# A graph layer's gather split between GpSimd and TensorE, with a maximum every second batch and direct stores

## The chip, the cores and the metric

The kernel runs on one core of one Trainium2 chip. The metric is device time in microseconds: the median of the runs. The kernel before takes 3633.04 us (3632.4 to 3636.79, three runs).

## The reference

Two graph layers, each followed by a layer norm; 6250 nodes with 16 features, 200000 edges sorted by destination. The change concerns the second layer:

```python
def _L1_gnn_ref(feat, efeat, W_msg, b_msg, W_attn, b_attn, src, dst):
    w_m = (efeat @ W_msg + b_msg).reshape(E, in_f, -1)
    w_a = (efeat @ W_attn + b_attn).reshape(E, in_f, -1)
    h_src = feat[src][:, :, None]
    e1 = w_m * h_src
    e2 = w_a * h_src
    seg_max = jax.ops.segment_max(e2, dst, num_segments=N)
    ex = jnp.exp(e2 - seg_max[dst])
    denom = jax.ops.segment_sum(ex, dst, num_segments=N)
    attn = ex / denom[dst]
    ft = jax.ops.segment_sum(e1 * attn, dst, num_segments=N)
    return ft.sum(axis=1)
```

`feat` is the first layer's output, x1 in the kernel (6272 x 16 with padding). Per edge there are two 16x16 matrices made from its attributes, each multiplied by the source node's row.

## The kernel before, in words

The first layer (to about 1600 us) is a loop over 196 batches of 1024 edges, one-hots and matmuls; the change adds only small work ahead of it. `update` then makes x1 and writes it to DRAM.

The second layer works on 197 batches of eight tiles of 128 edges, two tiles from each of four stretches of the edge list (S = 4). Its steps, each a small function:

- `gather(b)` (L579): eight indirect DMAs on GpSimd (L587), one a tile, fetch the source rows from x1 in DRAM into `hb`, two batches ahead (LEAD = 2).
- `load(b)` (L592): the edge attributes of two batches, on SP's queue.
- `multiply(b,u)` (L605): TensorE makes both matrices of two tiles in `pw` (two fp32r matmuls of 66x512, L613). There are three `pw` buffers, so it waits for `product` of three steps earlier.
- `maxima(b,u)` (L621): VectorE multiplies the attention half by the rows and takes the largest value of each partition into `cm`. `exps` (L628): ScalarE, exp of that minus a reference value, `neg[b]`. `message` (L632) and `product` (L637): VectorE, the other half times the rows, times the exp.
- `hot(b,..)` (L641): ScalarE makes one-hots of the destination within a window of R = 32 nodes, eight activations and one Relu.
- `add(b,0)` and `add(b,1)` (L681): TensorE adds the tiles into `acc` by the one-hots (L689, four windows side by side), and the carry from the batch before (L687).
- `leave(b)` (L692): ScalarE copies `acc`, of which there is one, to `sums`. `invert(b)` (L697): Ln and Exp on ScalarE, 1/denominator, written to `bank[:, 256:512]` (L701). `fold(b)` (L703): VectorE multiplies and reduces to 16 features per node.
- The reference value, every batch: `highest` (L652), VectorE; `across` (L656), a transpose on TensorE into `bank`; `top` (L659), VectorE, a maximum over it with the last `top`; `spread` (L667), TensorE, to all partitions; `refer` (L670), ScalarE, into `neg`; `carry` (L674), the factor between the two references.
- `store` (L713) and `put` (L718): every two batches the sums go to a DRAM log, and from there four DMAs a batch carry 32 nodes each to two tables at places read from a register. All are on SP's queue, and each `put` waits for the one before it on its table.

`bank` is one tile of PSUM of 512 columns, which `across`, `top`, `spread`, `refer`, `invert` and `fold` share in different ranges.

The order is written out by hand (L766 to L836), and each engine works through it in that order. In pass b the loop issues `new` work of batch b, `add` of batch b-1, and `leave`, `invert`, `fold` of batch b-2. On ScalarE the order is: leave, exps 0, invert, exps 1, hot 0-2, exps 2, refer, carry, hot 3-5, exps 3, hot 6-7. On TensorE: multiply 0, across, multiply 1, multiply 2, add 0, spread, multiply 3, add 1. On VectorE: maxima 0, message 0, maxima 1, top, message 1, product 0, maxima 2, message 2, product 1, maxima 3, message 3, product 2, fold, highest, product 3.

Three passes (12, 14, 16) also hold tests of the input (`checks`), each some 5 us. If one of these tests, or one at the end (`far_off`), finds that the assumptions on the data don't hold, a flag starts a slow general path.

Of the kernel before, what the change touches and what calls it, by code (L numbers as in the profile page):

```python
# [27 lines left out]
G = 8  # L28
# [4 lines left out]
S = 4  # L33
R = 32
LEAD = 2
RING = 16384
# [6 lines left out]
@with_exitstack  # L43
def gnn_kernel(ctx, tc, x_q, x_t4, src_p, dst_p, src_w, dst_w, prev_w, dst_r, base_h, src_q, dst_q, base_q, ea8_w, ea16, ea16_t,
               w_tp4, bd_w, w1_4, w1_msg, b1_msg, w1_attn, b1_attn, out):
# [16 lines left out]
    eas_dram = dram.tile([32, EP], F32, name="eas_dram")  # L62
    end_dram = dram.tile([32, 2 * W], F32, name="end_dram")
    tabs = [dram.tile([NP + W, D], F32, name=f"tab{k}_dram") for k in range(2)]

# [52 lines left out]
    with ExitStack() as l0:  # L118
# [24 lines left out]
        with tc.tile_pool(name="tab", bufs=2) as tabp, tc.tile_pool(name="tab1", bufs=1) as tab1, \  # L143
# [25 lines left out]
            for r in (16, 48):  # L169
# [14 lines left out]
                lambda: nc.vector.tensor_scalar(nsb, sb, -1.0, None, OP.mult),  # L184
            ]
            xhs = {}

# [303 lines left out]
    dwf, pwf, dqf, bqf = (t.bitcast(F32) for t in (dwi, pwi, dqi, bqi))  # L491
    step = keep.tile([W, NM], F32, name="step")

    def stretches():

        nc.vector.tensor_copy(dqf, dqi)
        nc.vector.tensor_copy(bqf, bqi)
        nc.vector.tensor_tensor(nrw.rearrange("p (m k) -> p m k", k=2), bqf.unsqueeze(2).to_broadcast([W, NM, 2]),
                                dqf.rearrange("p (m k) -> p m k", k=2), OP.subtract)
        nc.vector.memset(step[:, 0:S], -1000.0)  # L500
        nc.vector.tensor_tensor(step[:, S:NM], bqf[:, S:NM], bqf[:, 0:NM - S], OP.subtract)
        nc.vector.tensor_scalar(shiftw, step, float(R), 1000.0, OP.is_ge, OP.mult)
        nc.vector.tensor_tensor(step, step, shiftw, OP.add)
        sv = step.rearrange("p (b s) -> p b s", s=S)
        nc.vector.tensor_tensor(sv, sv, foot.unsqueeze(1).to_broadcast([W, NQ, S]), OP.add)
        nc.vector.tensor_scalar(shiftw, step, chan, None, OP.is_equal)

    def in_order():
# [14 lines left out]
    def fit_second():  # L523

        nc.vector.tensor_scalar(dqf, nrw, -float(R), None, OP.is_le)
        nc.vector.tensor_reduce(bad[:, 1:2], dqf, AX.X, OP.max)

        nc.vector.memset(step[:, 0:2 * S], 0.0)
        nc.vector.tensor_tensor(step[:, 1:S], bqf[:, 1:S], bqf[:, S + 1:2 * S], OP.is_equal)
        nc.vector.tensor_reduce(bad[:, 5:6], step[:, 0:S], AX.X, OP.max)  # L530
        nc.vector.tensor_tensor(step[:, S:2 * S - 2], bqf[:, 2:S], bqf[:, 1:S - 1], OP.subtract)
        nc.vector.tensor_scalar(step[:, S:2 * S - 2], step[:, S:2 * S - 2], R + 1.0, None, OP.is_le)
        nc.vector.tensor_reduce(bad[:, 6:7], step[:, S:2 * S - 2], AX.X, OP.max)
# [26 lines left out]
    with ExitStack() as l1:  # L560
        xp = l1.enter_context(tc.tile_pool(name="l_x", bufs=3))
        wp = l1.enter_context(tc.tile_pool(name="l_w", bufs=3))
        logp = l1.enter_context(tc.tile_pool(name="log", bufs=4, space=DRAM))
        psw = l1.enter_context(tc.tile_pool(name="l_psw", bufs=3, space=PSUM))
# [7 lines left out]
        x1n = keep.tile([W, NP // W, D], F32, name="x1n")  # L572
        nc.sync.dma_start(out=x1n, in_=x1_dram.rearrange("(p c) d -> p c d", p=W))
        checks = {12: in_order, 14: fit_first, 16: fit_second}
        st = {}

        bank = psm.tile([W, 512], F32, name="bank")

        def gather(b):  # L579

            st[b] = {"hb": []}
            st.pop(b - 8, None)
            for u in range(G // 2):
                hb = hp.tile([W, 2, D], F32, name="hb")
                for k in range(2):
                    t = b * G + 2 * u + k
                    nc.gpsimd.indirect_dma_start(  # L587
                        out=hb[:, k, :], out_offset=None, in_=x1_dram[:, :],
                        in_offset=bass.IndirectOffsetOnAxis(ap=srcq[:, t:t + 1], axis=0))
                st[b]["hb"].append(hb)  # L590

        def load(b):  # L592
# [6 lines left out]
            for r in (0, 32):  # L599
                to = ev[r:r + 32, :].bitcast(F32)  # L600
                nc.sync.dma_start(out=to.rearrange("r (s n) -> r s n", s=S)[:, 0:part.shape[1], 0:part.shape[2]], in_=part)
                if b == NQ - 1:
                    nc.sync.dma_start(out=to[:, (S - 1) * 4 * W:(S - 1) * 4 * W + 2 * W], in_=end_dram)

        def multiply(b, u):  # L605
# [46 lines left out]
        def highest(b):  # L652
            st[b]["m1"] = wp.tile([W, 1], F32, name="m1")
            nc.vector.tensor_reduce(st[b]["m1"], cm[:, b * S:(b + 1) * S], AX.X, OP.max)

        def across(b):  # L656
            nc.tensor.transpose(bank[0:1, 0:W], st[b]["m1"], ident)  # L657

        def top(b):  # L659

            before = st[b - 1]["top"] if b > 0 else None
            st[b]["top"] = wp.tile([1, 1], F32, name="top")
            nc.vector.tensor_reduce(st[b]["top"], bank[0:1, 0:W], AX.X, OP.max)
            if before is not None:
# [4 lines left out]

        def refer(b):  # L670

            nc.scalar.activation(neg[:, b:b + 1], bank[:, W:W + 1], AF.Copy, scale=-1.0)

        def carry(b):  # L674

            gap = wp.tile([W, 1], F32, name="gap")
            nc.scalar.activation(gap, neg[:, b - 1:b], AF.Exp, scale=-1.0, bias=neg[:, b:b + 1])
            nc.scalar.activation(cols[b % 3].rearrange("p (s r) -> p s r", r=R)[:, :, 0], shiftw[:, b * S:(b + 1) * S],
# [24 lines left out]
        def fold(b):  # L703
            v = st[b]
            r = wp.tile([W, 256], F32, name="q")
            nc.vector.tensor_tensor(r, bank[:, 256:512], v["sums"][:, 256:512], OP.mult)
            if b % 2 == 0:
                v["ft"] = wp.tile([W, 2, D], F32, name="ft")
            else:
                v["ft"] = st[b - 1]["ft"]  # L710
            nc.vector.tensor_reduce(v["ft"][:, b % 2, :], r.rearrange("p (i o) -> p o i", i=D), AX.X, OP.add)

        def store(b):  # L713

            st[b]["lg"] = lg = logp.tile([2, S, R * D], F32, name="lg")
            nc.sync.dma_start(out=lg.rearrange("k s (r d) -> (s r) k d", d=D), in_=st[b]["ft"])

        def put(b):  # L718

            rvs = nc.values_load_multi_w_load_instructions(  # L720
                bases_q[0:1, b * S:(b + 1) * S], engines=(mybir.EngineType.SP,), min_val=0, max_val=6249,
                skip_runtime_bounds_check_because="every dst is one of the 6250 nodes")[1]
            for s, rv in enumerate(rvs):
                if b < NQ - 3:
                    n, part = R, st[b | 1]["lg"][b % 2, s:s + 1, :]
                    nc.sync.dma_start(out=tabs[s % 2][ds(rv, n), :].rearrange("r d -> (r d)").unsqueeze(0), in_=part)
                else:
                    n = R if b < NQ - 1 else 1
                    nc.sync.dma_start(out=tabs[s % 2][ds(rv, n), :], in_=st[b]["ft"][s * R:s * R + n, b % 2, :])

        def clear():
# [4 lines left out]
            for s in range(1, S):  # L736
                rv = nc.values_load(bases_q[0:1, s:s + 1], engines=(mybir.EngineType.SP,), min_val=0, max_val=6249)
                nc.sync.dma_start(out=tabs[(s - 1) % 2][ds(rv + 1, R), :], in_=none)
                nc.sync.dma_start(out=tabs[s % 2][ds(rv, 1), :], in_=none[0:1, :])
# [11 lines left out]
        with tc.issue_after(tables.ins):  # L751
            for b in range(LEAD):
                gather(b)
            with tc.manual_schedule(engines=ORDERED | {mybir.EngineType.SP}):
# [8 lines left out]
                spread(0)  # L763
                refer(0)
                refer(1)
                for b in range(NQ + 2):  # L766
                    new, old, gone = b < NQ, 1 <= b <= NQ, b >= 2
                    trail = old and b + 1 < NQ
                    if b + LEAD < NQ:
                        gather(b + LEAD)  # L770
                    if b % 2 == 0:
                        if 2 <= b and b + 2 < NQ:
                            load(b + 2)
                        if 4 <= b and b - 3 < NQ - 3:
                            put(b - 4)
                            put(b - 3)
                    if new:
# [17 lines left out]
                    if new:  # L795
                        message(b, 1)
                        multiply(b, 2)
                        product(b, 0)
                    if old:
# [10 lines left out]
                    if trail:  # L810
                        refer(b + 1)
                    if b + 1 < NQ:
                        carry(b + 1)
                    if new:
                        hot(b, 3, 6)
                        maxima(b, 3)
                        exps(b, 3)
                        message(b, 3)
                        product(b, 2)
                        hot(b, 6, G)  # L820
                    if old:
                        add(b - 1, 1)
                    if gone:
                        fold(b - 2)
                        if b - 2 >= NQ - 3:
                            put(b - 2)
                        elif b % 2:
                            store(b - 2)
                    if new:
                        highest(b)  # L830
                        product(b, 3)
# [375 lines left out]
```

## Time and profile before

| | |
|---|---|
| median of three runs | 3633.04 us |
| the profiled execution: its own time | 3637.97 us |
| its span, first to last instruction | 3636.2 us |
| mean granted TensorE clock | 0.757 |
| busy: TensorE, VectorE, ScalarE, GpSimd | 3216.4, 3260.0, 2789.1, 1880.2 us |
| second layer, 1644.88 to 3586.24 us (194 batches): TensorE, VectorE, ScalarE, GpSimd busy | 1771.1, 1750.8, 1358.9, 1464.0 us of 1941.4 |
| mean clock there | 0.61 |
| gathers L587 | 1576, mean 946 ns |

The page shares busy time over the whole span, and the two layers differ much: the granted clock is 0.9 and more in nearly every slice of the first and 0.5 to 0.6 in the second. A busy TensorE at half clock needs twice the time for the same columns, so its busy time is to be read beside the clock. Stretches of single batches tell more than the sums. "Releaser" is what ended the idle time before an instruction.

### The profile page before, as it was taken

The page shows a single profiled execution, that of the slowest core. Times are in us where ns is not written, and L with a number is a line of the kernel's source. Part 1 is how long each engine was busy: PE and PEld are TensorE (multiplying, and loading weights), DVE is VectorE, ACT ScalarE, POOL GpSimd, SP SyncE. Part 2 cuts the span into 40 slices and gives each one's busy share as a digit, 9 for nine tenths or more (in the row PEclk, how much of TensorE's full clock was granted, in tenths as well). Part 3 has the DMA queues.
Part 4 walks back from the last instruction along what each step waited for, and adds up shares of the span by engine and source line. Part 5 has one row for each costly group of instructions (what it writes and reads, how often), then busy time and mean ns, then how long its engine had stood idle before and what let it go on. Part 6 is the DMA issues. An engine that isn't in the chain of part 4 may idle for free.

```text
span 3636.2 us, 53067 instructions
## 1 busy us (share of the span) xinstructions
PE 3216.4 (88%) x13725; PEld 2042.5 (56%) x13725; DVE 3260.0 (90%) x6470; ACT 2789.1 (77%) x5393; POOL 1880.2 (52%) x1792
## 2 busy tenths in 40 slices
PE   3999999999999999849799999999999999989995
PEld 3999989999999998823233333333333333333331
DVE  5999999999999999778989999999999998998986
ACT  4999999999999999716666777777777776776764
POOL 0222222222222222317777777777777777777773
PEclk9999999999999999955656666666665665565655
DMA  5433333333333333231121221212212122221211
GB/s 179 134 122 123 115 123 121 118 117 124 123 122 109 125 124 117 88 64 27 31 38 32 38 38 32 38 33 37 38 32 38 32 38 37 33 38 32 38 32 28
DMA packets 258415, 264.55 MB, mean 73 GB/s; under 512 B 105269, under 2 KB 193910, under 8 KB 258107
## 3 DMA queue, kind: packets, MB, share of 16 engines
q1 hardware_dynamic: 205931, 241.66, 22.8%
q0 software_dynamic: 50432, 13.01, 4.1%
q10 hardware_dynamic: 1744, 6.41, 0.6%
q8 instruction: 115, 1.88, 0.2%
q14 instruction: 193, 1.58, 0.1%
HBM read 223.67 MB, written 38.64 MB: 72 GB/s over the span
## 4 chain that ended last, share of the span: by engine, by line
PE 70%; DVE 14%; issue 7%; DMA 4%; ACT 3%; POOL 1%; SPq 0%; ACTq 0%; POOLq 0%; DVEq 0%
PE acc L348 32%; PE pw L613 13%; PE acc L689 12%; PE acc L687 6%; PE pm L283 5%; DVE xs L639 4%; DVE xs L624 3%; DVE pw L635 2%; DMA hb<-x_dram,srcq 2%; PE bank L668 1%; POOL hb L587 1%; ACT bank L701 1%; ACT r L700 1%; DMA xw_dram<-hl 1%; PE bank L657 1%
## 5 line engine op out<-in xcount | busy, mean ns | idle before, releaser
L587 POOL DMA_INDIRECT hb<-x_dram,srcq x1576 | 1490.4, 946 | 557.4 <-issue 269.4
L329 POOL TENSOR_TENSOR ll<-oa,sl 128x1024 fp32r<-128x1024 f32 x196 | 380.1, 1939 | 1146.1 <-DVE sl L336 1088.0
L630 ACT ACTIVATE xs<-xs,neg 128x512 f32<-128x512 f32 x788 | 562.6, 714 | 477.9 <-DVE cm L624 477.9
L613 PE MATMUL pw<-w,ev 66*128 66x512 f32 x1584 | 762.6, 610 | 77.7 <-DVE xs L639 59.7
L306 ACT ACTIVATE away<-iota,nsb 128x784 f32<-128x784 f32 x784 | 699.1, 939 | 5.9 <-DVE nsb L184 0.4
L689 PE MATMUL acc<-xs,oh 128*32 128x512 f32 x3152 | 687.7, 961 | 0.7 <-ACT sums L695 0.7
L613 PEld LDWEIGHTS pw<-w,ev 66*128 66x128 f32 x1584 | 375.0, 280 | 465.8 <-issue 340.4
L624 DVE CUSTOM_DVE_ANT_1 xs<-pw,hb 128x512 f32<-128x512 f32 x792 | 537.9, 679 | 91.0 <-PE pw L613 78.7
L308 ACT ACTIVATE oba<-away,one_t 128x3136 fp32r<-128x3136 f32 x196 | 572.7, 2922 | 6.4
L635 DVE TENSOR_TENSOR pw<-pw,hb 128x512 f32<-128x512 f32 x788 | 547.1, 694 | 20.5
L639 DVE TENSOR_TENSOR xs<-pw,xs 128x512 f32<-128x512 f32 x788 | 533.4, 677 | 0.0
L316 DVE TENSOR_SCALAR obd<-iota,sb 128x784 fp32r<-128x784 f32 x784 | 454.6, 622 | 0.0
L647 ACT ACTIVATE away<-iota,nrw 128x32 f32<-128x32 f32 x1576 | 389.6, 306 | 0.0
L348 PE MATMUL acc<-obd,ll 128*128 128x392 f32 x1568 | 346.6, 366 | 0.0
L687 PE MATMUL acc<-sums,col 128*128 128x512 f32 x392 | 340.6, 968 | 0.0
L348 PE MATMUL acc<-oba,ll 128*128 128x392 f32 x1568 | 326.1, 352 | 0.0
L283 PE MATMUL pm<-tw,ot 128*128 128x128 f32 x1568 | 214.5, 282 | 113.5 <-issue 89.9
L348 PE MATMUL acc<-obd,lh 128*128 128x392 f32 x1568 | 312.7, 341 | 1.0 <-DVE lh L329 1.0
L348 PE MATMUL acc<-oba,lh 128*128 128x392 f32 x1568 | 312.8, 341 | 0.0
L348 PEld LDWEIGHTS acc<-oba,ll 128*128 128x128 f32 x1568 | 298.8, 198 | 0.0
L689 PEld LDWEIGHTS acc<-xs,oh 128*32 128x32 f32 x3152 | 76.5, 135 | 382.7 <-issue 300.3
L348 PEld LDWEIGHTS acc<-obd,ll 128*128 128x128 f32 x1568 | 291.2, 202 | 0.0
(149 smaller groups left out, 3517.6 us busy)
## 6 DMA issues: line engine op xcount, KB each, us to landing
db<-in_dst_r SPq DMA_DIRECT2D x196, 512.0 KB
ev<-eas_dram SPq DMA_DIRECT2D x196, 256.0 KB
hb<-x_dram,srcq POOLq DMA_INDIRECT x1576
tw<-xw_dram SPq DMA_DIRECT2D x784, 32.0 KB
er<-in_ea_t SPq DMA_DIRECT2D x28, 448.0 KB
eas_dram<-eh SPq DMA_DIRECT2D x28, 448.0 KB
eas_dram<-el SPq DMA_DIRECT2D x28, 448.0 KB
tab_dram<-lg SPq DMA_DIRECT2D x776, 2.0 KB
```

The source lines that it names most:

```text
L306: nc.scalar.activation(v["away"][:, t, :], iota, AF.Abs, bias=nsb[:, b * G + t:b * G + t + 1])
L308: nc.scalar.activation(v["oba"], v["away"], AF.Relu, bias=one_t, scale=-1.0)
L316: nc.vector.tensor_scalar(v["obd"][:, t, :], iota, sb[:, n:n + 1], None, OP.is_equal)
L348: nc.tensor.matmul(acc[:, s, :B // 2], l[:, t].rearrange("p a h -> p (a h)"), ob[:, s * B // 2:(s + 1) * B // 2], start=b == 0 and t == GA ...
L587: nc.gpsimd.indirect_dma_start(out=hb[:, k, :], out_offset=None, in_=x1_dram[:, :], in_offset=bass.IndirectOffsetOnAxis(ap=srcq[:, t:t + 1 ...
L613: nc.tensor.matmul(pw[:, k].rearrange("p c n -> p (c n)"), ev[:, e:e + W], w1, start=True, stop=True)
L624: nc.vector.tensor_tensor_reduce(over(v["xs"][:, u, 0]), over(v[u][:, :, 0]), rows(b, u), 1.0, -2.0 * BIG, OP.mult, OP.max, cm[:, b * S + ...
L630: nc.scalar.activation(x, x, AF.Exp, bias=neg[:, b:b + 1])
L635: nc.vector.tensor_tensor(m, m, rows(b, u), OP.mult)
L639: nc.vector.tensor_tensor(x[:, u, 1], st[b][u][:, :, 1], x[:, u, 0], OP.mult)
L687: nc.tensor.matmul(v["acc"], cols[b % 3], st[b - 1]["sums"], start=False, stop=False)
L689: nc.tensor.matmul(v["acc"][s * R:(s + 1) * R, :], v["oh"][:, 2 * s + k, :], v["xs"][:, s, :, k, :], start=k == 0, stop=k == 1)
```

## The change

1. **Gather.** From batch 3 (PICK) GpSimd fetches seven tiles; the eighth comes from x1 in SBUF. There x1 lies as eight groups of 7 x 112 nodes: partition = node within 112, column block m (of seven), 8 x 16 columns for the eight groups; as two fp32r parts, `th` and `tl`. `places(b)` loads, on SP's queue, a row of 7 x 128 distances broadcast to 112 partitions (401 KB); `lows(b)` makes the one-hots `ox` of it on ScalarE (Abs and Relu over 112x896) at the end of the pass before; `pick(b)` adds 14 fp32r matmuls of 112x128 weights and 128 columns into `bank[:, 0:128]`; `choose(b)` takes the right one of eight groups on VectorE and writes the rows to `hb`.
2. **Preparation.** Twelve VectorE operations and eight DMAs ahead of the first layer write these distances to DRAM; `stretches` makes the group mask `which_h`; `table` splits x1.
3. **Maximum.** `highest`, `across`, `top`, `spread`, `refer` run every second batch and set two values of `neg`; the reference is up to one batch older. `across` and `top` use `bank[0:1, 128:256]`.
4. **Store.** `put(b-2)` follows `fold(b-2)` and writes 31 nodes (V) a window straight from SBUF; the log and `store` are gone.

The core of the diff:

```diff
+        def places(b):
+
+            xr[b] = xp.tile([X, 7 * W], F32, name="xr", bufs=2)
+            nc.sync.dma_start(out=xr[b], in_=xr_dram[b:b + 1, :].to_broadcast([X, 7 * W]))
+
+        def lows(b):
+
+            nc.scalar.activation(xr[b], xr[b], AF.Abs, bias=nchan[:X])
+            st[b]["ox"] = xp.tile([X, 7, W], F32R, name="ox", bufs=1)
+            nc.scalar.activation(st[b]["ox"].rearrange("p m e -> p (m e)"), xr.pop(b), AF.Relu, bias=one_t[:X], scale=-1.0)
+
+        def pick(b):
+
+            for m in range(7):
+                for k, t in enumerate((th, tl)):
+                    nc.tensor.matmul(bank[:, 0:8 * D], st[b]["ox"][:, m, :], t[:, m, :],
+                                     start=m + k == 0, stop=m + k == 7)
+
+        def choose(b):
+
+            g = wp.tile([W, 8, D], F32, name="g", bufs=2)
+            nc.vector.tensor_tensor(g, bank[:, 0:8 * D].rearrange("p (h d) -> p h d", d=D),
+                                    which_h[:, b, :].unsqueeze(2).to_broadcast([W, 8, D]), OP.mult)
+            nc.vector.tensor_reduce(st[b]["hb"][S - 1][:, 1, :], g.rearrange("p h d -> p d h"), AX.X, OP.add)
...
+            n = V if b < NQ - 1 else 1
             for s, rv in enumerate(rvs):
...
+                nc.sync.dma_start(out=tabs[s % 2][ds(rv, n), :], in_=st[b]["ft"][s * R:s * R + n, :])
...
-                    trail = old and b + 1 < NQ
+                    trail = old and b + 1 < NQ and b % 2 == 0
...
                         multiply(b, 2)
+                        if b >= PICK:
+                            pick(b)
                         product(b, 0)
...
                     if trail:
-                        refer(b + 1)
+                        refer(b + 1, 2)
...
                         hot(b, 3, 6)
+                        if b >= PICK:
+                            choose(b)
                         maxima(b, 3)
...
                         hot(b, 6, G)
+                        if PICK <= b + 1 < NQ:
+                            lows(b + 1)
...
                         fold(b - 2)
-                        if b - 2 >= NQ - 3:
-                            put(b - 2)
-                        elif b % 2:
-                            store(b - 2)
+                        put(b - 2)
+                    if PICK <= b + 2 < NQ:
+                        places(b + 2)
```

## The prediction

> **What bounds the kernel now.** First the engine times by stretch. The second layer's 197 batches begin 1644.88 us into the span (first start of `leave`, L695), and the 194 periods to 3586.24 take 1941.4 us: 10.01 each, or 9.93 without some 15 us of checks at batches 12, 14 and 16. I cut out three batches (start of `maxima(b,0)` to the next):
>
> ```profile
> core 0: us, PE busy (x) PEld busy (x) DVE busy (x) ACT busy (x) POOL busy (x), PEclk, DMA share, GB/s
> 2541.52:2551.71 10.19, 10.19 (x31) 3.90 (x29) 8.98 (x21) 7.02 (x20) 7.69 (x9) 0.50 0.07 7
> 2502.80:2512.26 9.46, 7.21 (x30) 2.53 (x29) 8.89 (x22) 6.91 (x20) 7.25 (x8) 0.80 0.09 9
> 2522.38:2531.93 9.55, 6.03 (x32) 2.39 (x30) 8.98 (x22) 6.92 (x20) 7.11 (x9) 1.00 0.09 8
> ```
>
> There are two regimes. At half clock TensorE is busy for all 10.19 us; at full clock it needs about 6 and VectorE sets 9.5. The mean clock of the 194 periods is 0.61, so most batches are of the first kind. GpSimd is near a third bound: eight gathers, 0.944 each and 0.30 between them, make 9.98 us, and it works almost without a break. But VectorE waits only 2.2 us in all for rows (wait table, 2000 to 3500), so it is a limit just below the other two.
>
> Next the chain in order of time, in a half-clock batch, then the timeline of the batch at 2502.80, where ScalarE and VectorE meet:
>
> ```profile
> 2542.21 1.71 PE pw L613 x4
> 2543.91 1.87 PE acc L689 x8
> 2545.78 0.51 PE bank L668 x2
> 2546.29 1.16 PE pw L613 x2
> 2547.45 1.71 PE acc L687 x2
> 2549.16 1.87 PE acc L689 x8
> 2551.03 1.15 PE pw L613 x2
> ```
>
> ```profile
> 2504.14 0.49 ACT L700 ACTIVATE r<-sums,tiny_t 128x256 f32<-128x256 f32 x1
> 2504.66 0.39 ACT L701 ACTIVATE bank<-r 128x256 f32<-128x256 f32 x1
> 2504.99 0.19 ACT L701 ACTIVATION_READ_ACCUMULATOR bank<-r 128x1 f32 x1
> 2505.20 0.28 DVE L663 TENSOR_REDUCE top<-bank 1x1 f32<-1x128 f32 x1 [0.40 <-ACT bank L701]
> ...
> 2509.49 0.71 ACT L630 ACTIVATE xs<-xs,neg 128x512 f32<-128x512 f32 x1
> 2510.10 0.52 ACT L647 ACTIVATE away<-iota,nrw 128x32 f32<-128x32 f32 x2
> ...
> 2510.65 0.51 ACT L650 ACTIVATE oh<-away,one_t 128x256 f32<-128x256 f32 x1
> 2511.06 0.58 ACT L695 ACTIVATE sums<-acc 128x512 f32<-128x512 f32 x1
> ```
>
> In the first, TensorE has no hole. In the second, `top` waits for `invert`'s write into another range of the same tile `bank`: waits on `bank` hold for the whole tile. And ScalarE passes without a break from `hot` to the next `leave`, which starts 1.2 us ahead of the next `maxima`.
>
> **TensorE: 14 matmuls more.** Nearest row: L283, also fp32r, 128x128 weights and 128 columns, at half and at full clock:
>
> ```profile
> 1085.79 1.94 PE L283 MATMUL pm<-tw,ot 128*128 128x128 f32 x8 [3.19 <-issue]
> 704.63 1.08 PE L283 MATMUL pm<-tw,ot 128*128 128x128 f32 x8
> ```
>
> Within the eight, starts lie 0.213 us apart at half clock and 0.111 at full, so `pick` costs 14 x 0.213 = 2.99 or 14 x 0.111 = 1.56. The Trainium skill (TensorE: Matmul & The Clock Gate, Back-to-back issue gap) gives about 0.081 for a load and matmul pair of 128 columns in a sustained stream: 1.13. I take the row; the rule's 0.4 us goes into the lower end. Halving `across` (0.21) and `spread` (0.51) returns 0.36. TensorE's half-clock batch is 10.19 + 2.99 - 0.36 = 12.8 if nothing else delays it.
>
> **VectorE.** `choose` adds a 128x128 multiply (the 128x256 one of L706 takes 0.413, so about 0.28) and a reduce over it (L711, twice as large, takes 0.584: 0.33 to 0.58); 0.6 to 0.86, I take 0.75. `top` (0.28 + 0.15, in the stream 0.39) and `highest` (0.06) go every second time. Without waits a batch is 9.46 - 0.40 (today's wait) = 9.06 now; then 9.06 - 0.06 + 0.75 = 9.75 for even and 9.06 - 0.39 + 0.75 = 9.42 for odd ones, mean 9.58.
>
> **ScalarE.** `lows` adds two 112x896 activations. L306 (784 elements) takes 0.939, L308 (3136) 2.922: 0.84 ns an element over 0.28, so 1.03 each, 2.06 together. It fits the total (7.0 + 2.06 - about 0.25 for the halved `refer` and `gap`), but the place decides: ahead of `leave`, which frees `acc` and starts `invert`. From `exps(b,3)` to the next `leave` are 2511.06 - 2509.49 = 1.57 now, then 3.63. From that `exps` (start = end of `maxima(b,3)`) to the next `maxima` are 2512.26 - 2509.43 = 2.8. `leave` then starts 0.83 after `maxima` instead of 1.2 before, and `exps(b,0)` waits behind it. I lay the batch out with `maxima` at 0: `leave` 0.83, `exps` 1.4, Ln 2.0, Exp 2.55, both done at X = 3.0 (now 2.4).
>
> **What waits on that.** The built order says what `pick` waits for: in odd batches the Exp of `invert(b-2)`, in even ones `top(b-1)`, which itself waits for that Exp. Queued behind `pick` are `add(b-1,0)`, `spread` and `multiply(b,3)`, which `maxima(b,3)` needs; from `maxima(b,3)` to the next batch are 3.5 us. At full clock (TensorE rows halved):
> - even: VectorE reaches `top` at 2.03, stalls to 3.0 (now 2.4); `pick` 3.35 to 4.95, `add` to 6.0, `spread` 6.4, `refer` 6.6, `choose` to 7.4 (it waits for `refer`), `maxima(b,3)` 7.4, period 10.9.
> - odd: `pick` 3.05 to 4.65, `add` to 5.7, `multiply(b,3)` to 6.45; `maxima(b,3)`, otherwise due at 5.9, starts there; period 10.0.
>
> Mean 10.45. At half clock, with the rows of the chain: even 3.35 + 3.0 + 1.87 + 0.51 + 1.16 = 9.9, and 3.5 more are 13.4; odd 3.05 + 3.0 + 1.87 + 1.16 = 9.1, so 12.6. Mean 13.0.
>
> **Which clock?** It changes in steps of 3.41 us. I added up, for each such step, the time in which matmul columns move. At full clock every step of layer two below 0.45 was followed by half clock (0.23 to 0.38 typically), all with 0.52 or more kept it. At half clock full speed came back after 0.84 and more, in layer one from 0.75; steps around L687 with no `spread` in them. `pick` moves columns only half of its time (0.053 of 0.111). In the full-clock layout TensorE idles from about 0.8, the end of `multiply(b,2)`, to 3.2. A step ending anywhere between 1.5 and 5.3 then has under 0.4; that stretch is longer than a step, so nearly every batch drops the clock once. Half clock then lasts two or three steps, till one lies in the dense part (`add`, `multiply`, L687, `add`, 6.6 us long). Followed by hand: a drop at 1.5 gives a 13.0 batch, the next step boundaries then miss the gap and give 10.4; a drop at 3.6 gives 12.65 and then 11.6. Averages 11.7 and 12.1; I take 11.75. The same page (Part 1) says that a busy step of some 3.4 us brings full clock and that activity releases the throttle: read alone, more matmuls would help, and the loop would run at 10.45. Against that stands the first row above: 10.19 busy of 10.19, and the clock at 0.50.
>
> **The rest.** `gather` loses one of eight: GpSimd 8.73 a batch, no gain while others set 10.4. SP: four direct stores a batch; the tail of today's run has eight such in 11.91 us, so 6 us a batch for four against 2 x 4.4 per two batches now. `places` is queued behind `put` and its fold: issued about 3.5 after the batch's start. The nearest row, db (512 KB broadcast), moves in 2.2 to 2.5 us; with issue and landing about 4, so the 401 KB are there at 7.5, before `lows` at 8.9. If late by 1 us, all of the batch is: +190 us. Layer one's twelve small VectorE operations and seven ACT DMAs (each third waits for a landing, about 8 us) lie in a hole: VectorE waits 12.3 us there for the first `pm`. `table` and its seven loads: 0 to +5 at the start of layer two; six operations in `stretches` (3.2 us) in a 4.0 us wait for rows. The tail has four stores less after the last fold: 0 to -6. Sum taken as 0.
>
> **Sum.** 194 x (11.75 - 9.93) = +353 us. The profiled execution is 3637.97 (span 3636.2 and 1.8 around it), so 3991; the median of the runs lies 4.9 below: 3986.
>
> **Rivals.**
> - Clock stays full (chance 0.20): 194 x 0.52 = +101: 3734. For it: `pick` fills part of today's gap. Against: half its time moves no columns, and `lows` moves the gap rather than closing it.
> - Clock stays half (0.14): 194 x 3.07 = +596: 4229. For it: today's 0.61. Against: 13 us is not near three steps (10.24) as 10.19 is, so the boundaries walk quickly into the dense part.
> - Faster (0.05): the waits on `bank` and behind `lows` vanish in other slack at full clock, VectorE's 9.58 sets the pace, GpSimd's 9.98 being gone: -68, 3565. It decides if `pick` starts by about 2.4 rather than 3.0 and the clock holds; the row 2511.06 (ScalarE has no gap there) speaks against it.
> - The change doesn't do what it says (0.01): a window over 31 nodes or a maximum two batches old sets the flag, and the general path runs, far outside any range. Destinations rise slowly, so I leave it.
> - The mixed clock (0.60): 3986, own range 3840 to 4140.
>
> The range 3730 to 4230 takes in full and half clock up to their middles. Beyond 0.2%, about what a measurement tells from no change: faster 0.05, same 0.02, slower 0.93.
>
> **What would show it.** Right: batches of 10 to 13.4 us with a mean near 11.75, the clock falling once in most batches during the gap before `pick`; `leave` starting behind the 112x896 pair, after `maxima(b,0)`; even batches longer than odd ones by 0.8, with VectorE waiting about 1 us at `top`; `pick` 1.6 or 3.0 long; GpSimd idle about 3 us a batch. Wrong: a steady clock over 0.9, `pick` starting right behind `multiply(b,2)`, or ScalarE waiting for `xr`.

## The result and the profile after

| | before | after |
|---|---|---|
| median of four runs each, one chip | 3632.72 us (3629.86 to 3636.79) | 4186.85 us (4179.08 to 4194.52) |
| span of the profiled execution | 3636.2 | 4177.3 |
| mean clock, all / second-layer loop | 0.757 / 0.61 | 0.786 / 0.687 |
| 194 periods of `leave`, total, mean | 1941.4, 10.01 | 2487.5, 12.82 |

The ratio is 1.153, 95% interval 1.151 to 1.154. The profiled execution grew by 541.1 us: the loop by 546.1, and what lies around it shrank by 5.0. So all of the loss is in the batches, at 2.8 us each, while the mean clock went up.

The runs in the last part of the experiments were made on three chips where the kernel before itself takes 4181 to 4189 us, so they are compared only with each other.

First the groups of the page, with mean duration and, behind the second bar, the idle time ahead of them:

```profile
L632 POOL DMA_INDIRECT hb<-x_dram,srcq x1382 | 1305.5, 945 | 1272.7 <-DVE pw L709 899.8
L669 PE MATMUL bank<-th,ox 112*128 112x128 f32 x1358 | 476.0, 368 | 380.2 <-DVE top L737 216.7
L698 DVE CUSTOM_DVE_ANT_1 xs<-pw,hb 128x512 f32<-128x512 f32 x792 | 540.8, 683 | 317.7 <-PE pw L687 309.5
```

GpSimd now waits for buffers (900 us): it is no limit. TensorE stands idle for 380 us ahead of `pick` (L669), 2 us a batch. VectorE waits 310 us for matmuls in `pw`. Next the stretches: an even and an odd batch, then one of the rare full-clock ones:

```profile
core 0: us, PE busy (x) PEld busy (x) DVE busy (x) ACT busy (x) POOL busy (x), PEclk, DMA share, GB/s
2801.14:2813.85 12.71, 10.43 (x44) 4.88 (x43) 9.66 (x24) 9.78 (x24) 6.59 (x7) 0.73 0.38 80
2813.85:2825.88 12.03, 10.48 (x43) 5.26 (x41) 9.35 (x22) 7.67 (x21) 6.60 (x7) 0.72 0.16 39
2022.81:2032.76 9.95, 7.30 (x43) 3.58 (x41) 9.23 (x22) 8.19 (x21) 6.42 (x7) 1.00 0.20 46
```

The same work takes 9.95 at full clock and 12 to 12.7 at a mean clock of 0.72. Before, a batch was either all slow with TensorE busy throughout, or nearly all fast. Now no engine is busy throughout, and hardly a batch is of either kind. The timeline of the even batch (maxima at 2801.14) shows how it begins:

```profile
2799.89 1.03 ACT L661 ACTIVATE xr<-xr,nchan 112x896 f32<-112x896 f32 x1
2800.96 1.04 ACT L663 ACTIVATE ox<-xr,one_t 112x896 fp32r<-112x896 f32 x1
2801.91 0.57 ACT L771 ACTIVATE sums<-acc 128x512 f32<-128x512 f32 x1
...
2803.52 0.39 ACT L777 ACTIVATE bank<-r 128x256 f32<-128x256 f32 x1
2803.84 0.19 ACT L777 ACTIVATION_READ_ACCUMULATOR bank<-r 128x1 f32 x1
2804.06 0.28 DVE L737 TENSOR_REDUCE top<-bank 1x1 f32<-1x128 f32 x1 [0.91 <-ACT bank L777]
...
2804.40 0.33 PE L669 MATMUL bank<-th,ox 112*128 112x128 f32 x1 [2.28 <-DVE top L737]
```

`leave` (L771) follows the pair of `lows` (L661, L663), 0.77 us after the maxima; the Exp is done at 2.9; `top` waits 0.91 for it; `pick` starts at 3.26 behind a hole of 2.28. TensorE's own rows of the odd batch, maxima at 2813.85, show what comes of it:

```profile
2816.30 0.33 PE L669 MATMUL bank<-th,ox 112*128 112x128 f32 x1 [1.55 <-ACT bank L777]
...
2818.83 0.41 PE L669 MATMUL bank<-tl,ox 112*128 112x128 f32 x1
2819.17 1.94 PE L765 MATMUL acc<-xs,oh 128*32 128x512 f32 x8
2821.04 1.22 PE L687 MATMUL pw<-w,ev 66*128 66x512 f32 x2
2822.05 1.73 PE L763 MATMUL acc<-sums,col 128*128 128x512 f32 x2
2823.72 1.06 PE L765 MATMUL acc<-xs,oh 128*32 128x512 f32 x8
```

The eight matmuls of `add` take 1.94 (half clock) right behind `pick` and 1.06 (full clock) at the end of the pass. By the trace's record of the clock, which changes in steps of 3.41 us, it fell at 2816.65, 0.35 us into `pick`, and rose at 2823.48. In between lies the serial stretch `pick`, `add`, `multiply(b,3)`, which `maxima(b,3)` waits for, and the carry (L763):

```profile
2819.28 0.29 DVE L675 TENSOR_TENSOR g<-bank,which_h 128x128 f32<-128x128 f32 x1 [0.15 <-PE bank L669]
2819.60 0.37 DVE L677 TENSOR_REDUCE hb<-g 128x16 f32<-128x128 f32 x1
2822.30 0.69 DVE L698 CUSTOM_DVE_ANT_1 xs<-pw,hb 128x512 f32<-128x512 f32 x1 [2.32 <-PE pw L687]
```

`choose` is short; then VectorE stands for 2.32 us. Cut at `maxima(b,0)`, over batches 12 to 189, in us and mean granted clock:

| kernel | batches | `pick` starts | `maxima(b,3)` | from there to next | period | clock in the gap | clock from `pick` to `maxima(b,3)` |
|---|---|---|---|---|---|---|---|
| changed | even | 3.20 | 9.14 | 4.40 | 13.54 | 0.98 | 0.59 |
| | odd | 2.51 | 8.54 | 3.64 | 12.17 | 0.91 | 0.53 |
| e1, Exp to SBUF | even | 2.36 | 9.15 | 4.61 | 13.76 | 0.65 | 0.50 |
| | odd | 0.96 | 6.52 | 3.70 | 10.22 | - | 0.83 |
| e4, `pick` later | even | 3.89 | 7.69 | 3.71 | 11.40 | 0.82 | 0.71 |
| | odd | 2.97 | 6.59 | 4.00 | 10.59 | 0.89 | 0.76 |
| e8, hole filled | even | 3.24 | 7.42 | 3.66 | 11.08 | 1.00 | 1.00 |
| | odd | 3.68 | 9.37 | 3.70 | 13.07 | 0.79 | 0.58 |

("Gap" is from 0.8 us after the batch's start to `pick`; in e1's odd batches it is hardly there and has no figure.) In the changed kernel the clock is full in the gap, where nothing runs, and near half where the batch's end is decided. In batches 12 to 189 it falls 168 times, and 166 of the 178 batches have a fall: 146 lie ahead of `pick` or within it, 20 between it and `maxima(b,3)`, two later.

What precedes each fall? The next table takes the 3.41 us ahead of each fall in the same batches, and names the matmuls ahead of which TensorE stood idle longest there (holes over 0.1 us):

| kernel | falls | longest hole ahead of |
|---|---|---|
| changed | 168 | `pick` 168 |
| e1, Exp to SBUF | 89 | `across` 57, `pick` 30, `multiply` 2 |
| e2, `lows` in mid-pass | 121 | `pick` 93, `multiply` 28 |
| e4, `pick` later | 95 | `spread` 44, `add` 30, `multiply` 10, `across` 9, `pick` 2 |
| e8, hole filled | 74 | `multiply` 74 |

In the changed kernel it is always the hole ahead of `pick`. Each later edit takes away part of these falls, and in what is left another hole comes first.

### The profile page after: what moved, and what is told of

The parts are those of the page before. It is cut to its first block, busy times and chain, and to the rows that moved or that the text cites. A ratio compares the mean times of both kernels' runs of the same rounds, so it can differ in the third digit from the quotient of the medians.

```text
span 4177.3 us, 58353 instructions
## 1 busy us (share of the span) xinstructions
PE 3539.7 (85%) x16147; PEld 2426.6 (58%) x16147; DVE 3368.4 (81%) x6583; ACT 3119.4 (75%) x5585; POOL 1695.2 (41%) x1598
## 4 chain that ended last, share of the span: by engine, by line
PE 67%; ACT 19%; DVE 6%; issue 6%; DMA 2%; POOL 0%; SPq 0%; ACTq 0%; DVEq 0%; POOLq 0%
PE acc L373 28%; PE bank L669 12%; PE acc L765 11%; PE pw L687 7%; PE pm L308 5%; ACT xs L704 4%; ACT ox L663 3%; DVE xs L698 3%; ACT xr L661 3%; PE acc L763 2%; ACT bank L777 2%; ACT r L776 2%; ACT sums L771 2%; ACT away L721 1%; PE bank L742 1%
## 5 line engine op out<-in xcount | busy, mean ns | idle before, releaser
L632 POOL DMA_INDIRECT hb<-x_dram,srcq x1382 | 1305.5, 945 | 1272.7 <-DVE pw L709 899.8
L669 PE MATMUL bank<-th,ox 112*128 112x128 f32 x1358 | 476.0, 368 | 380.2 <-DVE top L737 216.7
L765 PE MATMUL acc<-xs,oh 128*32 128x512 f32 x3152 | 669.4, 936 | 0.8 <-ACT sums L771 0.8
L687 PE MATMUL pw<-w,ev 66*128 66x512 f32 x1584 | 627.3, 515 | 22.2 <-DVE cm L698 17.4
L669 PEld LDWEIGHTS bank<-th,ox 112*128 112x128 f32 x1358 | 370.0, 272 | 467.2 <-DVE top L737 258.6
L687 PEld LDWEIGHTS pw<-w,ev 66*128 66x128 f32 x1584 | 313.3, 233 | 484.3 <-issue 410.1
L669 PE MATMUL bank<-tl,ox 112*128 112x128 f32 x1358 | 474.9, 365 | 0.0
L669 PEld LDWEIGHTS bank<-tl,ox 112*128 112x128 f32 x1358 | 380.4, 280 | 0.0
L763 PE MATMUL acc<-sums,col 128*128 128x512 f32 x392 | 352.1, 998 | 0.0
```

What stands on the lines that cost most here:

```text
L632: nc.gpsimd.indirect_dma_start(out=hb[:, k, :], out_offset=None, in_=x1_dram[:, :], in_offset=bass.IndirectOffsetOnAxis(ap=srcq[:, t:t + 1 ...
L669: nc.tensor.matmul(bank[:, 0:8 * D], st[b]["ox"][:, m, :], t[:, m, :], start=m + k == 0, stop=m + k == 7)
L687: nc.tensor.matmul(pw[:, k].rearrange("p c n -> p (c n)"), ev[:, e:e + W], w1, start=True, stop=True)
L765: nc.tensor.matmul(v["acc"][s * R:(s + 1) * R, :], v["oh"][:, 2 * s + k, :], v["xs"][:, s, :, k, :], start=k == 0, stop=k == 1)
```

## The experiments

Theory T: `pick` waits, through the shared tile `bank`, for an Exp that is late behind `lows`; the hole ahead of it drops the clock, and the serial stretch behind runs at half clock. Rivals: R1, the sheer load of 14 more matmuls; R2, the two ScalarE operations in front of `leave`; R3, the other parts of the change.

### The chip of 3631 us: one edit at a time

These four ran together; the kernel before took 3631.4 us beside them.

**e1: the Exp out of the shared tile.**

```diff
-            nc.scalar.activation(bank[:, 256:512], r, AF.Exp, scale=-1.0, accum_out=rsum[:, b:b + 1])
+            v["inv"] = r
+            nc.scalar.activation(r, r, AF.Exp, scale=-1.0, accum_out=rsum[:, b:b + 1])
...
-            nc.vector.tensor_tensor(r, bank[:, 256:512], v["sums"][:, 256:512], OP.mult)
+            nc.vector.tensor_tensor(r, v["inv"], v["sums"][:, 256:512], OP.mult)
```

> Edit: invert(b-2) writes its Exp into an SBUF tile instead of bank[:, 256:512]; all else as in the changed kernel (4187 us, batches of 12.82). In odd batches pick then waits only for the one-hots of lows, in even ones for top, which no longer waits for the Exp. Theory T (pick is late because of the shared tile, the hole before it drops the clock, and the serial stretch pick, add, spread, multiply(b,3) then runs at half clock): pick starts near 1.0 after maxima(b,0) in odd and 2.4 in even batches instead of 2.5 to 3.3; mean batch 10.8, 3800 us (3700 to 4000). Rival R1 (14 more matmuls on a TensorE that runs at half clock, 12.8 us of work a batch, wherever they wait): 12.4 to 12.8 a batch, 4110 to 4190. Rival R2 (two ScalarE operations ahead of leave, nothing else): leave stays late, 4187.

Measured: 4012.42 us, 1.105 of the kernel before (1.103 to 1.107); mean batch 11.97. That is 12 us above T's band and 98 below R1's, but the batches part. An even and an odd batch of this kernel, and the hole that ends the odd one:

```profile
core 0: us, PE busy (x) PEld busy (x) DVE busy (x) ACT busy (x) POOL busy (x), PEclk, DMA share, GB/s
2797.20:2810.94 13.74, 12.84 (x43) 6.66 (x42) 9.59 (x23) 9.99 (x24) 7.14 (x8) 0.51 0.34 73
2810.94:2820.55 9.61, 7.08 (x43) 3.68 (x41) 9.27 (x22) 7.45 (x20) 6.08 (x7) 1.00 0.16 48
```

```profile
2820.09 0.27 PE L731 MATMUL bank<-ident,m 128*1 128x128 f32 x1 [2.43 <-DVE m L728]
```

Both have the same 14 matmuls. In the odd one `pick` starts at 0.96 (mean), as T says; there the clock recovers, and the batch takes 9.61. In the even one, where `pick` still waits for `top` and starts at 2.36, TensorE is at half clock, busy for 12.84: the 12.8 of R1. So the load counts in full once the clock is half. What brings half clock here is mostly not the hole that T named: at the end of a full-clock odd batch TensorE stands for 2.43 us ahead of `across` (L731), waiting for `highest` (L728), and the clock falls at 2820.87, right behind. The Exp in `bank` is worth 174 us; the hole ahead of `across` took the place of the one ahead of `pick`.

**e2: `lows` in mid-pass.**

```diff
+                        if PICK <= b + 1 < NQ:
+                            lows(b + 1)
                         hot(b, 3, 6)
...
-                        if PICK <= b + 1 < NQ:
-                            lows(b + 1)
```

(With two buffers for `ox` and, for room, one for `q`.)

> Edit: lows(b+1) moves from the end of the pass to between carry and hot(b,3,6), so that leave and invert follow hot directly as in the kernel before. Theory T: leave starts about 1 us ahead of maxima(b,0) again, Exp of invert is done at 2.2 to 2.4 instead of 2.9, pick starts 0.5 to 0.9 earlier; the hole of TensorE stays over 1.4 us, so the clock still falls in most batches: 12.0 to 12.3 a batch, 4030 to 4090 us. R2 (the place of lows is the whole loss): the 2.06 us come back, 10.7 a batch, 3790. R1 (sheer TensorE load): no change, 4150 to 4190.

Measured: 4126.9 us, 1.137 (1.135 to 1.139); mean 12.52. `pick` starts at 2.76 and 2.44 instead of 3.20 and 2.51, and even batches' `top` waits 0.40 again instead of 0.91, but the clock still averages 0.69 and 0.50 from `pick` to `maxima(b,3)`. 60 us come back, somewhat less than T's 100 to 160 and far from R2's 400. R2 falls, also because e4 and e8 gain more and leave `lows` where it is.

**e4: `pick` behind `add` and `spread`.**

```diff
-                        if b >= PICK:
-                            pick(b)
...
                         spread(b - 1)
                     if new:
+                        if b >= PICK:
+                            pick(b)
```

> Edit: pick moves on TensorE from before add(b-1,0) to after add and spread, before multiply(b,3); same instructions, same number. add now fills the hole (it waits only for leave, done at 1.4), and pick finds the Exp nearly done. Theory T: the hole shrinks from 2.4 to under 1 us, the clock stays up in most batches, 10.2 to 10.8 a batch, 3680 to 3800 us. R1: TensorE has the same work, at half clock 12.8 a batch, 4120 to 4190. R2: leave is as late as before, 4187.

Measured: 3840.81 us, 1.059 (1.056 to 1.061); mean 10.97. An even and an odd batch:

```profile
core 0: us, PE busy (x) PEld busy (x) DVE busy (x) ACT busy (x) POOL busy (x), PEclk, DMA share, GB/s
2804.70:2815.42 10.72, 9.22 (x45) 4.54 (x43) 9.52 (x23) 8.80 (x23) 6.60 (x7) 0.84 0.42 93
2815.42:2824.97 9.55, 7.04 (x41) 3.45 (x41) 9.22 (x23) 8.28 (x21) 6.04 (x7) 1.00 0.21 50
```

The same instructions in another order: 346 us less. In full-clock odd batches VectorE sets 9.55. It is 41 above T's band and 279 below R1's: `add` in the hole does most of what T asks, but the clock still falls 95 times in 178 batches (0.71 and 0.76 behind `pick`), now mostly behind holes ahead of `spread` and `add`.

**e8: the hole filled with idle work.**

```diff
                         multiply(b, 2)
                         if b >= PICK:
+                            for _ in range(5):
+                                again(b, 2)
                             pick(b)
```

`again` is the two matmuls of `multiply(b,2)` once more, into the same place.

> Edit: the two matmuls of multiply(b,2) are issued five times more, with the same result, right behind multiply(b,2) and ahead of pick: 10 matmuls of 66x512 more a batch, 2.9 us at full and 5.7 at half clock. Nothing is left out. Theory T: they fill the hole of 2.4 us ahead of pick, the clock stays full, and pick, add, spread and multiply(b,3) run at full clock: the batch becomes shorter, 10.5 to 11.2, 3740 to 3870 us, although TensorE does more. R1: the load adds up: 12.8 + 2.9 to 5.7 = 15.7 to 18.5 a batch, 4740 to 5290.

Measured: 4034.11 us, 1.111 (1.109 to 1.113): 153 less than the changed kernel although TensorE does ten matmuls more. Mean 12.10. An even and an odd batch, and a hole at the start of the odd one:

```profile
core 0: us, PE busy (x) PEld busy (x) DVE busy (x) ACT busy (x) POOL busy (x), PEclk, DMA share, GB/s
3292.95:3303.72 10.77, 10.03 (x55) 5.95 (x53) 9.61 (x22) 8.60 (x23) 6.61 (x7) 1.00 0.35 91
3303.72:3317.66 13.94, 13.71 (x51) 8.28 (x51) 9.43 (x23) 8.40 (x21) 6.60 (x7) 0.63 0.14 35
```

```profile
3303.95 0.70 PE L687 MATMUL pw<-w,ev 66*128 66x512 f32 x2 [0.86 <-DVE xs L720]
```

No load theory allows a gain: R1 as the whole cause falls. Even batches are at full clock throughout, and `pick` starts no earlier (3.24), so the clock alone takes them from 13.54 to 11.08: the 89 even batches had 91 falls and now have 3. This is the run that shows the cause. In the odd batches the clock still falls (71 times in 89), and there the filler costs 0.9. T had expected all batches to be helped. In the odd batch shown the clock falls at 3305.45, in the filler itself; the only hole in the 3.41 us before is 0.86 us ahead of `multiply(b,2)`, which waits for a `pw` buffer. TensorE was busy for three quarters of that time, and it did not keep the clock.

### The chips of 4181 to 4189 us

There, batches of the kernel without `pick` already hold stretches in which VectorE waits for nothing that can be seen:

```profile
3023.38 0.68 DVE L713 TENSOR_TENSOR xs<-pw,xs 128x512 f32<-128x512 f32 x1
3027.18 0.69 DVE L698 CUSTOM_DVE_ANT_1 xs<-pw,hb 128x512 f32<-128x512 f32 x1 [3.12 <-issue]
```

From 1700 to 3500 us none of the four engines is busy for 117 us in all; in the kernel before on the first chip for 0.1. Its rows had landed and its matmuls had ended. But these stalls don't go with the time: they sum to 29 us in the run e14c below and to 0.4 in the changed kernel's own run on such a chip. The cause is open; the kernel before was not traced there.

**The change without its gather.**

```diff
-PICK = 3
+PICK = 1000
```

> Edit: PICK is set beyond the last batch, so that GpSimd fetches all eight tiles and places, lows, pick and choose never run; the maximum every second batch, the direct stores of 31 nodes and the preparation stay as changed. This measures parts 2 to 4 of the change without the gather. Theory T and R1 alike (all of the loss is in the gather): GpSimd's 8 x 1.247 = 9.98 us set the batch, TensorE needs 10.19 - 0.36 = 9.83 even at half clock: 9.98 to 10.05 a batch, 3625 to 3645 us. Rival R3 (the rarer maximum or the stores cost something themselves): over 3660.

Measured: 4163.33 us beside 4184.77, ratio 0.996 (0.994 to 0.997). Against R3, on such a chip: parts 2 to 4 cost nothing there and may give 0.4%. The forecast times were meant for a chip of the first kind, where R3 stays untested by itself; there e4, which keeps parts 2 to 4, is 209 us above the kernel before, so they have no more than that of the 554, unless `pick` in its later place gains something.

**Both moves (e1 and e4), with a filler, and with `lows` in mid-pass too.** The edits are those above; the filler is two repeats, not five.

> Edit: the two edits that took most together: Exp of invert into SBUF, and pick behind add(b-1,0) and spread. Measured so far: 4012 with the first alone (mean 11.97), 3841 with the second alone (10.97, of which full-clock even batches 10.81 with VectorE waiting 0.92 at top, odd ones 9.50). Theory T: the wait of top goes, full-clock batches become 9.9 and 9.5, and the clock falls somewhat less often: mean 10.2 to 10.4, 3680 to 3720 us. If the two edits only take away the same wait twice: 3841, no more. R1 (TensorE load at half clock, 12.8): over 3841.

> Edit: as in the run with both moves, and the two matmuls of multiply(b,2) issued twice more, same result, right behind it (4 of 66x512 more a batch: 1.1 us at full, 2.3 at half clock). The filler of ten alone took 153 us off in front of an unmoved pick, but its odd batches still dropped the clock. Theory T: the holes ahead of add and spread are filled, the clock stays at full nearly always, VectorE's 9.42 to 9.75 set the batch: 9.5 to 9.9, 3545 to 3625 us, below the kernel before. R1: 1.1 to 2.3 us a batch on top of the run with both moves: 210 to 450 us more than that one.

> Edit: as in the run with both moves, and lows(b+1) between carry and hot(b,3,6), so that leave comes before the start of the next maxima. That move alone took 60 us off (12.52 a batch), and its even batches took 11.5 us even at full clock, since ScalarE then delays exps(b,3) or refer. Theory T: add(b-1,0) need not wait for leave, the hole before it (0.5 us) closes; against it stand 2.06 us of ScalarE in the middle of the pass. Mean 9.8 to 10.6, 3600 to 3760 us. If the place of lows in mid-pass holds up exps(b,3): 10.6 to 11.2, worse than both moves alone.

Measured beside the same 4184.77: both moves 4070.29 (0.973, 0.970 to 0.976); with filler 4331.38 (1.037, 1.034 to 1.039); with all three moves 4082.0 (0.977, 0.975 to 0.980). The absolute numbers cannot be held against the forecasts, which were made for the other kind of chip. `lows` in mid-pass adds nothing to the two moves. The filler costs 261 us, against T, and 150 in the repeat below.

**Repeats, and the changed kernel beside them.**

> The kernel with both moves again, since the chip of the run before took 4185 us for the kernel before too, and all its engines stood still now and then for some 3 us at once, which no other trace here shows. Compared on a chip where the kernel before takes 3632. Theory T: mean 10.2 to 10.4, 3680 to 3720 us. The two edits take away the same wait twice: 3841. R1: over 3841.

Measured: 4062.66 beside 4180.92, 0.971 (0.968 to 0.975).

> The kernel with both moves once more. Its two runs so far were on chips where the kernel before takes 4181 to 4185 us. On a chip where that takes 3632: theory T: full-clock batches of 9.9 and 9.5, mean 10.2 to 10.4, 3680 to 3720 us. The two edits take away the same wait twice: 3841. R1: over 3841. On a chip of the slower kind it should repeat its ratio of 0.97 to the kernel before.

> Both moves and the filler of four matmuls once more, beside the run without it. On a chip where the kernel before takes 3632: theory T: the clock stays full nearly always, 9.5 to 9.9 a batch, 3545 to 3625 us; R1: 210 to 450 us more than the run without the filler. On a chip of the slower kind (measured there: 260 us more, mean clock 0.67 against 0.71) the filler should cost again, since stalls of other origin drop the clock there anyway.

Measured together: 4046.71 (0.969, 0.966 to 0.971) and 4196.59 (1.003, 1.002 to 1.005), beside 4184.22.

> The changed kernel itself once more, so that the runs made where the kernel before takes 4181 to 4185 us (both moves: 0.97 of it, both moves and filler: 1.00 to 1.04, no pick: 0.996) have the changed kernel beside them. If this chip is of that kind and theory T holds there: the changed kernel is above both moves by more than 200 us and takes 4300 to 4550, 1.03 to 1.09 of the kernel before. If the stalls there hide the hole ahead of pick: 4050 to 4200, no more than 1.00. If the chip takes 3632 for the kernel before: 4187, 1.15.

Measured on the same chip as the last two: 4291.06 beside 4188.61, 1.024 (1.022 to 1.026). That lies a little under T's 1.03 to 1.09 and over the rival's 1.00. So both moves together take 244 us off the changed kernel there (4046.71 against 4291.06), and are 3% below the kernel before on these chips. On the first kind of chip the two together were not run; e4 alone stays 5.9% above the kernel before there.

Why does the filler cost there? TensorE's groups over 1660 to 3700 us, without and then with it, idle time behind the second bar:

```profile
L687 PE MATMUL pw<-w,ev 66*128 66x512 f32 x1351 | 558.8, 521 | 161.4 <-DVE xs L713 82.3 <-issue 51.9 <-DVE pw L709 25.0
L765 PE MATMUL acc<-xs,oh 128*32 128x512 f32 x2700 | 519.9, 851 | 70.3 <-ACT sums L771 65.3 <-issue 2.2 <-ACT ox L663 0.9
L742 PE MATMUL bank<-top,ones_row 1*128 1x1 f32 x170 | 37.6, 288 | 39.2 <-DVE top L739 38.3 <-DVE top L737 0.8
```

```profile
L687 PE MATMUL pw<-w,ev 66*128 66x512 f32 x1256 | 533.9, 533 | 168.1 <-DVE xs L720 139.9 <-issue 18.2 <-DVE pw L716 9.0
L772 PE MATMUL acc<-xs,oh 128*32 128x512 f32 x2516 | 482.8, 846 | 2.9 <-ACT sums L778 2.5
L749 PE MATMUL bank<-top,ones_row 1*128 1x1 f32 x158 | 36.6, 298 | 1.0 <-DVE top L746 0.7 <-DVE top L744 0.3
```

It filled its own holes (70.3 and 39.2 became 2.9 and 1.0), but the idle time ahead of the `multiply` matmuls stayed (161.4 and 168.1). The loop's mean clock did not rise (0.709 and 0.701), and at half clock the filler is load. In the 3.41 us ahead of its 89 falls the longest hole was ahead of `multiply` 68 times and ahead of `across` 21 times, never ahead of `add` or `spread`. So the falls follow holes that the filler did not touch; no run filled these, so that they are the cause is not shown.

## Why the prediction was right, and its one wrong term

Direction, place and mechanism held; of the 554 us, 353 were forecast. The number held only in the wide range: 4187 lies outside the 3840 to 4140 of the mixed clock, the case that came, and inside 3730 to 4230 because that range was drawn to take in the rivals too. To that extent it was luck. The mis-sized term is the mean batch, 11.75 us. Without the three passes with `checks` it is (2487.5 - 15) / 194 = 12.74, so that 194 x (12.74 - 9.93) = 545 in place of 353.

- **Where `pick` starts.** Forecast 3.35 and 3.05, measured 3.20 and 2.51. Exp done at 3.0 against 2.9, `leave` at 0.83 against 0.77. `top`'s wait: 3.0 - 2.03 = 0.97 against 82.0 us over 97 times, 0.85. Right for even batches; odd ones start half a microsecond earlier than laid out.
- **The batch at one clock.** Forecast for full clock: 10.9 and 10.0. In e8's full-clock batches (from `leave` to `leave`, medians) 88 even ones take 11.03 and 15 odd ones 9.99; the changed kernel's own rare ones 9.95. For half clock: 13.4 and 12.6; measured, with the clock down behind `pick` but mostly up elsewhere in odd batches (0.81 from `maxima(b,3)` on), 13.54 and 12.17. Right within 0.45.
- **Which clock: the step that failed.** "The next step boundaries then miss the gap and give 10.4", and with it the averages of 11.7 and 12.1. They do not miss it. From batch 2 on, three batches in all took under 10.05. The clock falls in 166 of 178 batches, and mostly ahead of or within `pick`, so the stretch behind is near half clock (0.59 and 0.53) on average. It is enough that the clock is down there: the batch then comes near the half-clock layout (mean 13.0), although the loop's mean clock is 0.69. I had counted a share of half clock over the batch; it had to be counted over the serial stretch alone. (The step from "11.7 and 12.1" to 11.75 was not reasoned either: their middle is 11.9, 29 us more.)
- **The parts of the 545.** With full clock throughout, the layout's 10.45 would give 194 x 0.52 = 101; the other 444 are then the clock. This split is an estimate from the layout, which e8's full-clock batches bear out.
- **Even and odd.** Forecast 0.8 to 0.9 apart; measured 1.37 (13.54 and 12.17).
- **The limit of moving columns.** The prediction read from the kernel before that a step with 0.52 or more keeps full clock. That does not carry over: counted in the same way (a 66x512 matmul as 0.213 us at full clock), the steps ahead of e8's falls have up to 0.74. A limit that holds for all these kernels was not found.
- **The load rule.** For the Trainium skill's sentence that activity releases the throttle (TensorE: Matmul & The Clock Gate, Part 1) I had put the loop at 10.45 and set it aside. More matmuls did not help as `pick`, behind a hole; as filler in the hole they brought even batches to 11.03 at full clock. So activity kept full clock there; e8's odd batches, three quarters busy, lost it, and the row that I set against the rule, 10.19 busy at a clock of 0.50, says that activity does not always bring it back.
- **Small terms.** `choose` 0.29 + 0.37 = 0.66 (forecast 0.75); `lows` 1.03 + 1.04 (1.03 each). Four direct stores take 2.1 to 2.4 us, not 6; `xr` was never late. GpSimd brought nothing, as forecast. All outside the loop: -5.0 (forecast 0, with -6 to 0 for the tail).
- **Rivals.** Half clock throughout (4229) came nearest in time, by another way: full clock where nothing depends on it. Full clock throughout (3734) did not come. `pick` never started by 2.4 in even batches, so the faster case had no chance.

## What to carry to other kernels

Where an engine's clock follows its load, a wait costs more than its length: ask what runs right behind the hole, and count the clock over that stretch, not over the batch. Moving the same 14 matmuls behind work that was ready gave back 346 of 554 us, and taking one activation's output out of the shared tile 174. Then look for the next hole: each edit here left falls behind another one. A filler helped in the batches where it closed the hole (e8's even ones) and cost where the clock fell all the same, since there it is load at half clock.

## What was not expected of the hardware

- Ten more matmuls a batch made the kernel 153 us faster (e8).
- A hole of 1.5 to 2.3 us ahead of matmuls that move columns only half of their time goes with half clock in 166 of 178 batches. With the filler in its place, a hole of about 0.87 us elsewhere went ahead of every fall in e8.
- One and the same kernel, the one before, took 3632 us on one chip and 4181 to 4189 on three others, and the order of versions changes with it: both moves are below the kernel before on those, while the changed kernel is 1.15 of it on one kind and 1.02 on the other. Its cause stays open.
